# Which images of a normalised convolution take the combined path, and which engine measures them: four in eight and none on VectorE, to three in eight and one in eight on VectorE

## The chip, the cores and the metric

One Trainium2 chip, one core of it. The metric is the device time of one execution in microseconds (us). Engine names: PE is TensorE, DVE is VectorE, ACT is ScalarE, POOL is GpSimd, SP is SyncE, whose queue issues the loads and stores.

## The reference

`x` holds 160 images of 128 channels, 32x32 pixels, in f32. Images are dealt out to five weight sets (`b n` order, 32 images for each set). Every image is normalised over groups of four channels, run through a 3x3 convolution, and added to itself:

```
def _gn(v, G=32, eps=1e-5):                 # mean and variance of 4 channels x 32 x 32
    ...
    return ((g - m) / jnp.sqrt(s + eps)).reshape(v.shape)

# weights: U is quantised in two steps, s1 = (max - min)/3, s2 = s1/5
v1 = s1 * floor(U / s1);  v2 = s2 * floor((U - v1) / s2);  w = v1 + v2
x = x + conv3x3(_gn(x), w)                  # 128 -> 128 channels, padding 1, 5 weight sets
```

## The kernel before

**One image at a time.** Channels lie on the 128 partitions, an image is 1024 numbers on each. The normalised image is fed to PE in two f16 parts, a high part (the image rounded to f16) and a low part (what the rounding left), both multiplied by the same f16 weights. All weights are made beforehand, three columns of taps (`COLS`) for each weight set, and doubled, which is why the end multiplies by 0.5.

**Two paths for an image.** Two neighbouring output rows can share products: with the row differences, the pair sums and the pair differences of the input, four row products do the work of six. The kernel always feeds the low part in this form. The high part goes one of two ways:

- A *direct* image: ACT normalises it into f32 (`z`, L511) and rounds it (`hi`, L519). DVE subtracts (`lo`, L574) and builds the low part's differences and sums (`rows`, L588 to L591). PE runs the nine plain taps of `hi` (L614) and the shared products of `rows` (L640).
- A *combined* image: POOL writes two border rows (`outer_rows`, L539 and L540) and DVE the other differences and sums of the raw image (`combine`, `v`, L550 to L556). ACT scales and rounds all 2048 numbers (`vh`, L561), and DVE takes what is left (`vl`, L567). PE runs only shared products, of both parts (L640).

`combined(i)` (L522) says which: images 14 to 155 whose number modulo 8 is in `COMBINED`. With (1, 3, 5, 7) these are 71 of the 160 images; the other 89 are direct.

**PE's order.** `conv(i)` first issues the pair products of image i+1 into the PSUM tile `m` (`sums_of_pairs`), then the rest of image i into its tile `eo`. In between lie two small matmuls for each group's statistics (`means`, `variances`) and the turning of new weights (`turn_column`). `m` has one buffer and `eo` two, so before PE can start the pair products of image i+2, DVE must have read `m` of image i+1.

**What happens in stage i of the loop** (L857 to L961), engine by engine, in program order. The program is scheduled by hand: each engine runs its instructions in the order in which they are written.

- ACT: the first half of measuring image i+14, its sum (`image_sum`, L192); `sum` of image i-1, half of `eo` (L720); `m2` of image i+1, the copy of half of `m` (`leave`, L696); then `vh` or `z` and `hi` of image i+3; the second half of the measuring (`image_square`, L199); small operations for group statistics.
- DVE: the low part of image i+2 (`vl`, or `lo` and `rows`); one step of the next weight set's quantisation (`take(later, 1)`); `pairs` of image i+1 (L705, L706), which adds `m` and `m2` into `eo` and so frees `m`; then `combine` of image i+4 if that is a combined one, otherwise a second quantisation step; and last the measuring of those images that `by_vector` gives it.
- POOL: the transfer that adds `sum` to the image in SBUF (`accumulate`, L733); `outer_rows` of image i+4; the statistics of a group.
- SP: stores and loads, in units of two images; loads run 20 images ahead.

The lead of measuring is 14 images in the steady part and starts at about 10. Until stage 10 every second stage therefore measures two images instead of one. Statistics are made for groups of eight images (smaller groups at the start), two stages after the last image of a group is measured.

**Who measures.** `by_vector(i)` (L485) is true for images from 8 on whose number modulo 8 is in `MEASURED`; before, that tuple is empty. Such an image is measured on DVE by `Statistics.image` (L175): two `bn_stats` over 512 numbers, one `bn_aggr`, and two small multiplications, at the end of the stage.

Of the kernel before, what the change touches and what calls it, by code (L numbers as in the profile page):

```python
# [309 lines left out]
class Main:  # L310
# [24 lines left out]
    STAT_LEAD = 14  # L335
    LOAD_LEAD = 20
    STEADY = 14
    COMBINED = (1, 3, 5, 7)
    MEASURED = ()
    EARLY = 8  # L340
    FIRST = 3

# [142 lines left out]
    def by_vector(self, i):  # L485
        return i >= self.EARLY and i % 8 in self.MEASURED

# [34 lines left out]
    def combined(self, i):  # L522

        return self.STEADY <= i < self.imgs - LAST and i % 8 in self.COMBINED

# [485 lines left out]
```

## Time and profile before

| | |
|---|---|
| time, median of 3 runs | 1009.54 us (1009.02 to 1009.97) |
| the profiled execution's own time | 1009.54 us |
| its span in the profile | 1007.8 us, so 1.7 us lie around the span |
| mean granted PE clock | 0.995 of full |
| busy time PE, DVE, ACT, POOL | 964.8, 886.5, 931.2, 369.5 us |
| weight loads of PE (PEld) | 575.6 us |
| images combined, direct | 71, 89 |
| images measured by ACT, by DVE | 160, 0 |

The busy time of an engine is the union of its instructions' times. Matmuls overlap each other in the profile, so the pace of PE is read from start to start and not from the length of a matmul. The profiled execution took the median time, so a sum that starts from 1009.54 us stands for both.

### The profile page before, as it was taken

The page shows a single profiled execution, that of the slowest core. Times are in us where ns is not written, and L with a number is a line of the kernel's source. Part 1 is how long each engine was busy: PE and PEld are TensorE (multiplying, and loading weights), DVE is VectorE, ACT ScalarE, POOL GpSimd, SP SyncE. Part 2 cuts the span into 40 slices and gives each one's busy share as a digit, 9 for nine tenths or more (in the row PEclk, how much of TensorE's full clock was granted, in tenths as well). Part 3 has the DMA queues.
Part 4 walks back from the last instruction along what each step waited for, and adds up shares of the span by engine and source line. Part 5 has one row for each costly group of instructions (what it writes and reads, how often), then busy time and mean ns, then how long its engine had stood idle before and what let it go on. Part 6 is the DMA issues. An engine that isn't in the chain of part 4 may idle for free.

```text
span 1007.8 us, 15892 instructions
## 1 busy us (share of the span) xinstructions
PE 964.8 (96%) x5910; PEld 575.6 (57%) x5910; DVE 886.5 (88%) x1197; ACT 931.2 (92%) x1279; POOL 369.5 (37%) x555
## 2 busy tenths in 40 slices
PE   1879999999999999999999999999999999999997
PEld 0435456665666665666666566666665666666663
DVE  7956689999999999989999999999999988888873
ACT  4899999999999999999999999999999999998660
POOL 3413162534425243524243444415243623333210
PEclk9989999999999999999999999999999999999999
DMA  9627889999999999999999999999999999997763
GB/s 361 238 84 188 210 233 260 261 260 270 270 274 293 272 270 261 257 274 286 269 290 260 266 265 277 291 286 262 264 254 262 289 266 275 268 256 191 180 176 129
DMA packets 67287, 254.42 MB, mean 252 GB/s; under 512 B 5248, under 2 KB 5248, under 8 KB 67200
## 3 DMA queue, kind: packets, MB, share of 16 engines
q1 hardware_dynamic: 45168, 173.09, 50.4%
q0 software_dynamic: 22032, 80.23, 40.9%
q8 instruction: 48, 0.79, 0.3%
q14 instruction: 39, 0.32, 0.1%
HBM read 89.19 MB, written 83.89 MB: 172 GB/s over the span
## 4 chain that ended last, share of the span: by engine, by line
PE 88%; ACT 7%; issue 2%; DVE 1%; POOL 1%; DMA 1%; SPq 0%
PE eo L614 30%; PE eo L640 28%; PE m L640 28%; ACT junk L199 2%; ACT z L511 1%; ACT junk L192 1%; ACT hi L519 1%; ACT sum L720 1%; DMA range<-in_L_conv_U_dram 1%; DVE ext L422 1%; DVE ext L423 1%; ACT m L696 0%; PE pg L225 0%; PE m L614 0%; PE pg L208 0%
## 5 line engine op out<-in xcount | busy, mean ns | idle before, releaser
L640 PEld LDWEIGHTS <-wt 128*128 128x128 f16 x4104 | 400.3, 98 | 240.1 <-DVE rows L590 7.8
L614 PE MATMUL eo<-hi,wt 128*128 128x496 f16 (+3 forms) x1584 | 381.8, 377 | 1.1 <-ACT wt L476 1.1
L733 POOL DMA_DIRECT2D xt<-sum x153 | 135.9, 888 | 462.8 <-ACT sum L720 443.1
L614 PEld LDWEIGHTS <-wt 128*128 128x128 f16 x1656 | 162.9, 100 | 156.7 <-issue 4.5
L199 ACT ACTIVATE junk<-xt,mv 128x1024 f16<-128x1024 f32 x160 | 183.3, 1146 | 0.4
L192 ACT ACTIVATE junk<-xt 128x1024 f16<-128x1024 f32 x160 | 169.1, 1057 | 14.1 <-DMA xt<-in_x_dram 10.7
L705 DVE TENSOR_TENSOR eo<-m,m 128x512 f32<-128x512 f32 x157 | 109.2, 696 | 76.2 <-ACT m L696 75.8
L567 DVE SCALAR_TENSOR_TENSOR vl<-v,rstd,vh 128x2048 f16<-128x2048 f32 x71 | 166.7, 2348 | 3.5 <-ACT vh L561 3.5
L720 ACT ACTIVATE sum<-eo 128x1024 f32<-128x1024 f32 x153 | 154.1, 1007 | 12.9 <-PE eo L640 12.9
L640 PE MATMUL eo<-vl,wt 128*128 128x248 f16 (+1 forms) x852 | 162.9, 273 | 0.0
L640 PE MATMUL eo<-vh,wt 128*128 128x248 f16 (+1 forms) x852 | 162.9, 273 | 0.0
L640 PE MATMUL m<-vh,wt 128*128 128x496 f16 (+1 forms) x426 | 161.8, 380 | 0.0
L640 PE MATMUL m<-vl,wt 128*128 128x496 f16 (+1 forms) x426 | 161.7, 380 | 0.0
L640 PE MATMUL eo<-rows,wt 128*128 128x248 f16 (+1 forms) x1032 | 155.6, 273 | 0.0
L561 ACT ACTIVATE vh<-v,rstd 128x2048 f16<-128x2048 f32 x71 | 143.0, 2014 | 0.0
L640 PE MATMUL m<-rows,wt 128*128 128x512 f16 x516 | 127.0, 383 | 9.5 <-DVE rows L590 7.3
L706 DVE TENSOR_TENSOR eo<-m,m 128x512 f32<-128x512 f32 x157 | 109.8, 700 | 5.4
L574 DVE TENSOR_TENSOR lo<-z,hi 128x1024 f16<-128x1024 f32 x89 | 108.9, 1224 | 5.9 <-ACT hi L519 5.8
L511 ACT ACTIVATE z<-xt,shift,rstd 128x1024 f32<-128x1024 f32 x89 | 110.7, 1244 | 1.3 <-POOL shift L242 1.3
L696 ACT COPY m<-m 128x512 f32<-128x512 f32 x157 | 91.2, 581 | 20.4 <-PE m L640 17.8
L519 ACT CAST hi<-z 128x1024 f16<-128x1024 f32 x89 | 93.0, 1045 | 2.8
L550 DVE TENSOR_TENSOR v<-xt 128x960 f32<-128x960 f32 x71 | 81.7, 1150 | 0.0
(105 smaller groups left out, 804.3 us busy)
## 6 DMA issues: line engine op xcount, KB each, us to landing
xt<-in_x_dram SPq DMA_DIRECT2D x78, 1024.0 KB, 9.1
out_dram<-xt SPq DMA_DIRECT2D x78, 1024.0 KB, 5.0
xt<-sum POOLq DMA_DIRECT2D x153, 512.0 KB, 6.8
range<-in_L_conv_U_dram SPq DMA_DIRECT2D x4, 576.0 KB, 6.9
u<-in_L_conv_U_dram SPq DMA_DIRECT2D x4, 576.0 KB, 11.5
xt<-in_x_dram SPq DMA_DIRECT2D x4, 512.0 KB, 9.4
out_dram<-xt SPq DMA_DIRECT2D x3, 512.0 KB, 3.0
u<-in_L_conv_U_dram SPq DMA_DIRECT2D x2, 288.0 KB, 3.1
```

The costliest lines, as they stand in the source:

```text
L192: self.nc.scalar.activation(junk, image, ACTF.Copy, scale=-1.0 / image.shape[1], accum_out=self.mv[:, j, 0:1],)
L199: self.nc.scalar.activation(junk, image, ACTF.Square, bias=self.mv[:, j, 0:1], accum_out=self.mv[:, j, 1:2],)
L511: nc.scalar.activation(z, self.image(i), ACTF.Identity, bias=st.shift[:, j : j + 1], scale=st.rstd[:, j : j + 1],)
L561: self.nc.scalar.mul(vh, self.v[i], st.rstd[:, j])
L567: self.nc.vector.scalar_tensor_tensor(vl, self.v[i], st.rstd[:, j], self.hi[i], ALU.mult, ALU.subtract)
L574: self.nc.vector.tensor_sub(lo[:, 1 : self.H + 1, :].rearrange("p h w -> p (h w)"), self.z.pop(i), self.hi[i].rearrange("p h w -> p (h w)"),)
L614: nc.tensor.matmul(target[:, h, r0 - h0 : r1 - h0, c0:c1], self.wts[n, col][:, k, :], tile[:, s0 : s0 + r1 - r0, c0 + dw : c1 + dw], start ...
L640: self.nc.tensor.matmul(target[:, :, c0:c1], self.wts[n, col][:, kind, :], source[:, :, c0 + dw : c1 + dw], start=start, stop=stop, skip_g ...
L705: nc.vector.tensor_add(rows[:, :, 0], m[:, 0], m2)
L706: nc.vector.tensor_sub(rows[:, :, 1], m[:, 0], m2)
L720: nc.scalar.mul(self.sum[i], eo, 0.5)
L733: self.nc.gpsimd.dma_start(self.image(i), self.sum.pop(i), accum_op=ALU.add)
```

## The change

Two constants of the class `Main` change; nothing else in the file does.

```
-    COMBINED = (1, 3, 5, 7)
-    MEASURED = ()
+    COMBINED = (1, 4, 6)
+    MEASURED = (5,)
```

By the rules above, 53 images are combined and 107 direct (71 and 89 before). Images 15, 17, 19, 21 and so on used to alternate with direct ones; now the pattern of eight is direct, combined, direct, direct, combined, direct, combined, direct, starting with image 14. Images 13, 21, 29 and so on to 157, 19 in all, are measured on DVE and no longer on ACT.

## The prediction

> **What bounds the kernel now.** I began with the page's busy times and the chain that ended last.
>
> ```profile
> PE 964.8 (96%) x5910; PEld 575.6 (57%) x5910; DVE 886.5 (88%) x1197; ACT 931.2 (92%) x1279; POOL 369.5 (37%) x555
> PE 88%; ACT 7%; issue 2%; DVE 1%; POOL 1%; DMA 1%; SPq 0%
> ```
>
> Three engines are nearly full, and PE carries 88% of the chain. With engines this close, I need to know which one sets the pace of a pair of images, so I read the timeline for the start of each piece of PE's work: pair products of a direct image, rest of a combined one, pair products of a combined one, rest of a direct one, and the next piece.
>
> ```profile
> 514.95 1.46 PE L640 MATMUL m<-rows,wt 128*128 128x512 f16 x6
> 516.25 0.38 PE L640 MATMUL eo<-vh,wt 128*128 128x256 f16 x2
> 518.88 0.38 PE L640 MATMUL m<-vh,wt 128*128 128x512 f16 x1
> 521.47 1.43 PE L614 MATMUL eo<-hi,wt 128*128 128x512 f16 x6
> 526.59 0.60 PE L640 MATMUL m<-rows,wt 128*128 128x512 f16 x2
> ```
>
> From start to start: 1.30, 2.63, 2.59 and 5.12 us. A direct image costs PE 1.30 + 5.12 = 6.42 us, a combined one 2.59 + 2.63 = 5.22, a pair 11.64. Is that PE's own pace, or does ACT hold it there? The end of the run answers: from about 915 us on there is nothing left to measure, and ACT waits.
>
> ```profile
> 925.84 1.02 ACT L720 ACTIVATE sum<-eo 128x1024 f32<-128x1024 f32 x1 [2.72 <-PE eo L640]
> 937.62 1.02 ACT L720 ACTIVATE sum<-eo 128x1024 f32<-128x1024 f32 x1 [2.64 <-PE eo L640]
> 949.26 1.02 ACT L720 ACTIVATE sum<-eo 128x1024 f32<-128x1024 f32 x1 [2.64 <-PE eo L640]
> ```
>
> ACT sits idle 2.6 us before each of these, and still the pair takes 937.62 to 949.26 = 11.64 us. So PE is the bound, and ACT was only just keeping up. In the start-up it was the other way about. PE's timeline there shows the only waits after 70 us:
>
> ```profile
> 100.81 1.47 PE L640 MATMUL m<-rows,wt 128*128 128x512 f16 x6 [0.26 <-DVE eo L706]
> 107.92 1.47 PE L640 MATMUL m<-rows,wt 128*128 128x512 f16 x6 [0.52 <-DVE eo L706]
> 115.12 1.47 PE L640 MATMUL m<-rows,wt 128*128 128x512 f16 x6 [0.61 <-DVE eo L706]
> 122.23 1.47 PE L640 MATMUL m<-rows,wt 128*128 128x512 f16 x6 [0.52 <-DVE eo L706]
> 129.43 1.47 PE L640 MATMUL m<-rows,wt 128*128 128x512 f16 x6 [0.30 <-DVE eo L706]
> ```
>
> These are direct images, 7.0 to 7.2 us apart instead of 6.42. DVE is named, but it had waited for ACT's `m2`, and ACT runs without a gap here because it measures three images in two stages.
>
> **Part 1: 18 images become direct.** 71 - 53 = 18 images cost PE 6.42 - 5.22 = 1.20 us more each. All of them lie where PE sets the pace (it has no wait after 136 us), so nothing hides it: **+21.6 us**. The small matmuls for statistics and weights stay as many. POOL loses 18 times two border rows (0.70 + 0.82 us); POOL is 37% busy, so that is worth nothing.
>
> **Part 2: 19 images leave ACT.** The rows of what goes, of the nearest row to what comes, and of the quantisation step used below:
>
> ```profile
> L199 ACT ACTIVATE junk<-xt,mv 128x1024 f16<-128x1024 f32 x160 | 183.3, 1146 | 0.4
> L192 ACT ACTIVATE junk<-xt 128x1024 f16<-128x1024 f32 x160 | 169.1, 1057 | 14.1 <-DMA xt<-in_x_dram 10.7
> L422 DVE TENSOR_REDUCE ext<-u 128x1 f32<-128x576 f32 x2 | 1.5, 748 | 2.8 <-DMA u<-in_L_conv_U_dram 2.8
> L422 DVE TENSOR_REDUCE ext<-range 128x1 f32<-128x1152 f32 x4 | 5.4, 1346 | 0.6 <-DMA range<-in_L_conv_U_dram 0.6
> L109 DVE SCALAR_TENSOR_TENSOR tt<-nn,s2nlo,tt 128x384 f32<-128x384 int16 x15 | 9.2, 613 | 0.1
> ```
>
> With the accumulator reads (0.19 each, half hidden), a measured image takes ACT about 2.4 us, so ACT gives up 19 x 2.4 = 46 us and gets back 18 x 0.3 (`z` and `hi` take 2.2 us from start to start, `vh` 1.9). In the steady part that only lengthens ACT's waits. In the start-up it counts. Images 13 and 21 are measured in stages 3 and 8, before and inside the stretch that ACT holds; they take 4.8 us out of ACT's chain, of which about 0.5 is lost at once because ACT catches up with PE. PE's stages 7 to 13 run from 93.97 to 143.02, 49.05 us; as pure work they are 7 x 6.42 + 0.6 for statistics and one turned column = 45.5. ACT's credit of 4.3 exceeds this 3.5, so the gain is PE's whole excess, less a little for a stage that does not close up: **-3.3 us** (bounds 0 and -3.5). What is late next is PE itself.
>
> **Part 3: DVE's new measuring.** The trace has no `bn_stats`. By the two reduce rows an element costs (1346 - 748)/576 = 1.04 ns, so 512 elements 0.68 us; two of them 1.36. The three small operations go by the 128x1 rows of the start (0.15 us, 0.06 to 0.12 from start to start). Bounds: 2 x 0.44 + 0.2 = 1.1 us (each like the f16 subtraction of 512, 439 ns) and 2 x 1.35 + 0.5 = 3.1 us (each as long as the 1152-element reduce). I take 1.6, near the f32 reduce. It comes last in stages with i mod 8 = 7, and behind it are the low part of image i+3 and all else that PE waits for. Its image was loaded six images, over 30 us, earlier and lands in 9 us, so it should wait for no transfer. Per eight images DVE has 3 x 4.62 (combined) + 5 x 2.41 (direct) + 8 x 1.33 (`pairs`) + 1.6 = 38.2 us and up to 13 quantisation steps of 0.54, 45.2 in all, against PE's 5 x 6.42 + 3 x 5.22 + 0.55 = 48.3. On average DVE has room.
>
> **Part 4: the new rhythm.** A stage of PE is the rest of image i and the pair products of i+1. Before, long (5.12 + 2.59 = 7.71 us) and short stages (2.63 + 1.30 = 3.93) alternated. Now residues 0 to 7 take 7.71, 3.93, 6.42, 7.71, 3.93, 7.71, 3.93, 6.42. Each `pairs(i+1)` has to end before stage i+1 begins. The order on ACT and DVE in residues 4 to 6 is the tight place, and I add it from start-to-start times of the timeline:
>
> - Stage 4 is short, with 6.27 us on ACT after its `sum` starts: 1.34 to `m2`, 0.46, `z` 1.27, `hi` 0.95, the square 1.20, the next sum 1.05. ACT enters stage 5 late by 6.27 - 3.93 = 2.34.
> - In stage 5 `sum` (0.91) and `m2` (0.59) let `pairs` start 3.84 after the stage; DVE goes on with `pairs` 1.33, `combine` 2.36, the direct low part for stage 6 at 2.41, a quantisation step 0.54, `pairs` again 1.43, and 0.12 until PE takes it: 12.03.
> - Stages 5 and 6 last 7.71 + 3.93 = 11.64 on PE.
>
> So PE waits about 0.4 us for `pairs` where a quantisation step lies in between. Steps run through roughly 26 of 32 images of the first four sets, which hits stages 22, 38, 46, 54, 70, 78, 86, 102, 110 and 118: ten waits, **+4.0 us**. Without the step there is none, and with steps of 0.35 to 0.71 us it is 0.2 to 0.6, so 2 to 6 us. A second tight place, stage 1, follows DVE's unbroken run from there; it comes to 29.7 us against PE's 29.7, and costs nothing unless the measuring takes longer than 1.6. This stage's wait would be the one that appears next.
>
> Sum: 1009.5 + 21.6 - 3.3 + 4.0 = **1031.8 us**.
>
> One rule speaks against reading it like this. The Trainium skill, "Perfetto Trace Analysis", section "Identifying the Most-Contended Engine", says that matmul busy time is no measure of how full PE is and that the load of weights is, and to work on the engine with the highest occupancy. By that, PE stands at 57%, ACT at 92% is the one to relieve, and taking 46 - 5 = 41 us from it would give about 968 us. I take neither busy figure for PE, but the distance from start to start, which stays at 11.64 us when ACT is idle.
>
> **Rivals.**
>
> - *No new wait on PE.* If ACT enters stage 5 earlier than I added, the ten waits vanish: 1009.5 + 21.6 - 3.3 = 1027.8. For it: 0.4 us is small against the sums it comes from. Against: I dropped nothing that would make it shorter. 20%.
> - *DVE becomes the bound in the measured stages.* If the measuring takes 2.6 us instead of 1.6, stage 1 waits 1.0 us more in the ten blocks with quantisation steps, giving 1042; if the start-up gain is also missed, 1045. For it: 45 of 48 us are already full. 10%.
> - *Faster: ACT is the bound.* Then PE has slack to take the 1.20 us, and the run goes with ACT's 41 us, to 968. The point from which it decides is a direct image that costs PE less than 3.3/18 = 0.18 us more than a combined one, since otherwise the added PE work outweighs the start-up. The trace shows 1.20. 2%.
> - *Nothing moves.* The change was described as another order on ACT and POOL and a last image taken bank by bank; the diff has none of this, only two tuples. If the images taken from the combined path did not reach PE's chain, the time would stay at 1009.5. The chain is 88% PE, so 1%.
>
> **How the numbers follow.** The forecast of 1031.8 has 67%. The range of 1026.5 to 1039 takes in the case without waits and the bounds of the waits and the start-up, and leaves out the long measuring, both small rivals and mishaps that I did not think of. A measurement of this kernel tells 0.2%, about 2 us, from no change: faster 0.02, same 0.01, slower 0.97.
>
> **What would show it.** L561 with 53 instances and L511 with 107; a stretch of eight images at 48.3 us instead of 47.0, with PE at 100% and ACT near 92%; ACT waiting on PE before `sum` all along; no wait of PE for L706 between 100 and 130 us, and about ten of 0.2 to 0.6 us later. `bn_stats` at about 0.68 us. It would be wrong if ACT stayed gapless, if PE showed repeated waits of 1 us for L590 or L706, or if the eight-image stretch stayed at 47.

## The result, and the profile after

The changed kernel took 1038.93 us (median; 1038.7 to 1040.11) against 1009.75 us for the kernel before in the same comparison: 1.0289 times as long, 95% interval 1.0271 to 1.0307. The forecast was 1031.8 us, in a range of 1026.5 to 1039.0. The sign and the mechanism were right, but the time lies only 0.07 us inside the upper edge of the range, and one of the four terms was less than half of what came. The profiled execution took 1038.94 us with a span of 1037.2, 29.4 us more than the span before.

The page's busy times and the chain that ended last, of the changed kernel:

```profile
PE 987.3 (95%) x5910; PEld 575.3 (55%) x5910; DVE 879.3 (85%) x1292; ACT 901.0 (87%) x1221; POOL 344.2 (33%) x519
PE 74%; DVE 12%; ACT 11%; issue 2%; DMA 1%; POOL 0%; SPq 0%; ACTq 0%; DVEq 0%
```

ACT is 30 us less busy and DVE 7, and the kernel is 29 us slower. PE's share of the chain fell from 88 to 74%: DVE and ACT now hold the chain in places. The start-up, in PE's timeline (start, duration), answers to the five waits of 0.26 to 0.61 us before:

```profile
94.87 1.46 PE L640 MATMUL m<-rows,wt 128*128 128x512 f16 x6
...
101.29 1.46 PE L640 MATMUL m<-rows,wt 128*128 128x512 f16 x6
...
107.71 1.46 PE L640 MATMUL m<-rows,wt 128*128 128x512 f16 x6
```

Those waits are gone, and direct images follow one another at 6.42 us. The waits of PE in the whole run (what waited, for whom, us, times, longest) and the groups of the new measuring and of ACT's `sum`:

```profile
PE m L640 <- DVE eo L706: 6.7, 11, 0.9
L182 DVE BATCH_NORM_STATS2 st<-xt 128x6 f32<-128x512 f32 x38 | 24.3, 681 | 0.0
L184 DVE BATCH_NORM_AGGREGATE both<-st 128x2 f32<-128x12 f32 x19 | 4.0, 209 | 0.7
L720 ACT ACTIVATE sum<-eo 128x1024 f32<-128x1024 f32 x153 | 155.3, 1015 | 38.4 <-PE eo L640 38.3
```

ACT now waits 38 us for PE before `sum` (13 before), and the list has eleven waits of PE for `pairs`, all of them after 190 us (shorter ones, of 0.15 us and less, are not in it). The signs named ahead came: `vh` (L561) has 53 instances and `z` (L511) 107, and eight images take 48.0 to 49.3 us instead of 47.0. One sign of being wrong, repeated waits of 1 us for L706, came near: four of the waits are 0.8 to 0.9 us in the list, and these stages last 0.95 to 1.05 us longer than their work.

To see where the span went I took, from PE's timeline, the start of every stage (its first pair product) and compared its length with the pieces of the prediction, 1.30, 2.63, 2.59 and 5.12 us, plus the small matmuls in it:

| part of the span | before | after | difference |
|---|---|---|---|
| up to stage 4 | 74.30 | 75.19 | +0.89 |
| stages 4 to 12 | 62.13 | 58.65 | -3.48 |
| stages 13 to 157 | 852.67 | 883.81 | +31.14 |
| the rest | 18.7 | 19.6 | +0.86 |

Of the 31.14, 21.6 is the work of 18 images, and 9.5 is left over. Added up stage by stage, the excess over work is 9.7 us, and it lies in 16 stages, all with i mod 8 = 6: 22, 30, 38 and so on to 142. The first and the last row are not shown to be the change's. PE runs the same instructions up to stage 4 in every kernel here that measures images 8 to 12 on ACT, and its stage 4 began anywhere from 74.3 to 76.6 us in their profiles. At the end both traces agree to 0.01 us until the last store is issued, 13.4 us after the start of stage 158; the 0.86 lies in the closing semaphores behind it.

### The profile page after: what moved, and what is told of

The parts are those of the page before. It is cut to its first block, busy times and chain, and to the rows that moved or that the text cites. A ratio compares the mean times of both kernels' runs of the same rounds, so it can differ in the third digit from the quotient of the medians.

```text
span 1037.2 us, 15844 instructions
## 1 busy us (share of the span) xinstructions
PE 987.3 (95%) x5910; PEld 575.3 (55%) x5910; DVE 879.3 (85%) x1292; ACT 901.0 (87%) x1221; POOL 344.2 (33%) x519
## 3 DMA queue, kind: packets, MB, share of 16 engines
q1 hardware_dynamic: 45168, 173.09, 49.3%
## 4 chain that ended last, share of the span: by engine, by line
PE 74%; DVE 12%; ACT 11%; issue 2%; DMA 1%; POOL 0%; SPq 0%; ACTq 0%; DVEq 0%
PE eo L614 34%; PE m L640 21%; PE eo L640 18%; ACT junk L199 2%; ACT z L511 2%; ACT m L696 2%; DVE lo L574 2%; DVE eo L706 2%; ACT hi L519 2%; DVE eo L705 1%; ACT sum L720 1%; ACT junk L192 1%; DVE v L550 1%; DVE rows L588 1%; DVE v L553 1%
## 5 line engine op out<-in xcount | busy, mean ns | idle before, releaser
L614 PE MATMUL eo<-hi,wt 128*128 128x496 f16 (+1 forms) x1908 | 458.7, 377 | 1.1 <-ACT wt L476 1.1
L640 PE MATMUL eo<-rows,wt 128*128 128x248 f16 (+1 forms) x1248 | 188.1, 273 | 0.0
L640 PE MATMUL m<-rows,wt 128*128 128x496 f16 (+1 forms) x624 | 153.4, 382 | 14.4 <-DVE rows L590 7.3
L192 ACT ACTIVATE junk<-xt 128x1024 f16<-128x1024 f32 x141 | 149.0, 1056 | 13.4 <-DMA xt<-in_x_dram 11.2
L511 ACT ACTIVATE z<-xt,shift,rstd 128x1024 f32<-128x1024 f32 x107 | 133.6, 1248 | 0.0
L567 DVE SCALAR_TENSOR_TENSOR vl<-v,rstd,vh 128x2048 f16<-128x2048 f32 x53 | 124.5, 2348 | 6.2 <-ACT vh L561 5.8
L640 PE MATMUL eo<-vh,wt 128*128 128x248 f16 (+1 forms) x636 | 121.6, 273 | 0.0
L640 PE MATMUL eo<-vl,wt 128*128 128x248 f16 (+1 forms) x636 | 121.6, 273 | 0.0
L640 PE MATMUL m<-vh,wt 128*128 128x496 f16 (+1 forms) x318 | 120.7, 380 | 0.0
L640 PE MATMUL m<-vl,wt 128*128 128x496 f16 (+1 forms) x318 | 120.7, 380 | 0.0
L706 DVE TENSOR_TENSOR eo<-m,m 128x512 f32<-128x512 f32 x157 | 109.8, 700 | 5.4
L561 ACT ACTIVATE vh<-v,rstd 128x2048 f16<-128x2048 f32 x53 | 106.4, 2007 | 0.0
L588 DVE TENSOR_TENSOR rows<-lo 128x1024 f16<-128x1024 f16 x104 | 71.6, 688 | 1.3
```

Source lines behind the costliest of these rows:

```text
L192: self.nc.scalar.activation(junk, image, ACTF.Copy, scale=-1.0 / image.shape[1], accum_out=self.mv[:, j, 0:1],)
L511: nc.scalar.activation(z, self.image(i), ACTF.Identity, bias=st.shift[:, j : j + 1], scale=st.rstd[:, j : j + 1],)
L567: self.nc.vector.scalar_tensor_tensor(vl, self.v[i], st.rstd[:, j], self.hi[i], ALU.mult, ALU.subtract)
L614: nc.tensor.matmul(target[:, h, r0 - h0 : r1 - h0, c0:c1], self.wts[n, col][:, k, :], tile[:, s0 : s0 + r1 - r0, c0 + dw : c1 + dw], start ...
L640: self.nc.tensor.matmul(target[:, :, c0:c1], self.wts[n, col][:, kind, :], source[:, :, c0 + dw : c1 + dw], start=start, stop=stop, skip_g ...
L706: nc.vector.tensor_sub(rows[:, :, 1], m[:, 0], m2)
```

## The experiments

Each was compared with runs of the kernel before on its own chip, which took 1011.1 us (first four), 1011.2 (next four) and 1010.8 (last two). The differences below are against these; for the changed kernel the difference is +29.2 us.

**The pattern alone.**

```
-    COMBINED = (1, 3, 5, 7)
+    COMBINED = (1, 4, 6)
```

> Only COMBINED changes to (1, 4, 6); ACT still measures all images. Theory A (the time after is 21.6 us of PE work, minus a start-up gain of 2.6 to 3.3 that comes from the measuring of images 13 and 21, plus about 9.7 us of waits in stages with i mod 8 = 6 that come from the pattern itself): the start-up gain is lost and the waits stay, so about 1041.5 us, 1040 to 1044, with PE's waits for L706 back at 100 to 130 us. Theory B (the waits come from the bn_stats on DVE): the waits vanish, about 1031 us.

Measured: 1042.41 us, 31.3 more; ratio 1.0305, interval 1.0288 to 1.0322. PE's timeline has the start-up waits again, for example

```profile
116.16 1.47 PE L640 MATMUL m<-rows,wt 128*128 128x512 f16 x6 [0.61 <-DVE eo L706]
...
123.27 1.47 PE L640 MATMUL m<-rows,wt 128*128 128x512 f16 x6 [0.52 <-DVE eo L706]
```

and the excess in stages 6 mod 8 is 9.7 us, stage for stage within 0.01 that of the changed kernel, plus 0.4 in stage 14. So the waits come from the pattern and not from `bn_stats`, which this kernel does not run.

**The measuring alone.**

```
-    MEASURED = ()
+    MEASURED = (5,)
```

> Only MEASURED changes to (5,); images 1, 3, 5, 7 modulo 8 stay combined. Theory A: PE's work stays, the start-up closes up by 2.6 to 3.3 us, DVE is at about 46.9 of 47.0 us for eight images and just fits: 1007 us, 1006 to 1011. Theory B: the measuring on DVE makes PE wait about 0.5 us in each of the 13 blocks of eight with quantisation steps: 1010 less 3 plus 6.5, 1013 or more.

Measured: 1017.12 us, 6.0 more; ratio 1.0053, interval 1.0037 to 1.0070. Theory A fell here. The start-up closed up (stages 4 to 12 took 58.64 us), but PE then lost 9.2 us from stage 13 on, 0.1 to 0.7 in each of 19 stages, most of them 1 mod 8. DVE's timeline around stages 23 to 25 of this kernel (start, duration) shows why:

```profile
200.73 1.15 DVE L550 TENSOR_TENSOR v<-xt 128x960 f32<-128x960 f32 x1
...
203.06 1.28 DVE L182 BATCH_NORM_STATS2 st<-xt 128x6 f32<-128x512 f32 x2
204.37 0.21 DVE L184 BATCH_NORM_AGGREGATE both<-st 128x2 f32<-128x12 f32 x1
...
204.75 1.22 DVE L574 TENSOR_TENSOR lo<-z,hi 128x1024 f16<-128x1024 f32 x1
...
208.15 0.70 DVE L706 TENSOR_TENSOR eo<-m,m 128x512 f32<-128x512 f32 x1
```

DVE has no gap from `combine` to the `pairs` that ends at 208.85, and PE starts stage 25 at 208.90. The measuring took 203.06 to 204.75 = 1.69 us, as estimated; but with four combined images in eight, DVE has no such 1.7 us to spare while quantisation steps run. The last such wait is in stage 121; the measuring goes on to stage 143, but the last quantisation is done, and there are no more. A sum of 46.9 of 47.0 us was no room at all: the order in which the work has to be ready left less than the mean.

**The start-up alone.** Only images 13 and 21 are measured on DVE:

```
-        return i >= self.EARLY and i % 8 in self.MEASURED
+        return i in (13, 21)
```

> As the kernel before, but images 13 and 21 alone are measured on DVE. Theory A: the whole start-up gain and nothing else, 1007 us (1006 to 1007.5), with no wait of PE for L706 between 100 and 130 us. Rival (ACT's credit is used up elsewhere, or the start-up gain in the changed kernel came from image 14 being combined): 1009 to 1010 us.

Measured: 1007.29 us, 3.8 less; ratio 0.9964, interval 0.9951 to 0.9977. Stages 4 to 12 took 58.65 us, the same as in the changed kernel to 0.01, and PE's timeline shows no wait between 70 and 160 us. The gain in the start-up comes from these two images.

**The quantisation step and the copies moved.** The changed kernel, with work put off and none left out:

```
-            take(later, 1)                     # between lo and rows
+            if i % 8 != 6: take(later, 1)      # in stages 6 mod 8: behind pairs
...
-            for column, pt in turned: ...      # two ACT copies of a turned column
+            if i % 8 != 4: ...                 # else in the next stage
```

> The changed kernel with two moves: in stages with i mod 8 = 6 the quantisation step in front of pairs goes behind pairs, and the two copies of a turned weight column on ACT (0.73 us) are put off by a stage where they would fall in a stage with i mod 8 = 4. No work is added or removed. Theory A (PE's waits there are ACT's lateness plus DVE's row of work): the waits of 9.7 us in 16 stages fall to about 16 x 0.16, so 1032 us (1031 to 1034). Rival (PE waits there for another reason, such as the single buffer of m alone): 1038 to 1039.

Measured: 1035.50 us, 24.4 more; ratio 1.0236, interval 1.0219 to 1.0253. That misses the expected 1031 to 1034: all excess was to fall to about 2.6 us, and it fell from 9.7 to 6.8. Stages 38, 46, 70, 78, 102 and 110 went to 0.16. But stages 22, 30, 54, 62, 86, 94 and 126 ended at 0.56 (118 at 0.84), and a few stages 1 mod 8 now take 0.2 too long: a copy that is put off from stage 4 to stage 5 makes ACT late for stage 6 instead. The next run tests that.

**The copies clear of both stages.** As above, with the copies held in stages 4 and 5, and the last column of a set finished two stages earlier so that its copies fall in a stage 3 mod 8:

```
-            if i % 8 != 4: ...
+            if i % 8 not in (4, 5): ...
...
-            if b == self.per_set - 4:
+            if b == self.per_set - 6:
                 run(later)
```

> As the run with the quantisation step and the copies moved, but the copies of a turned column now also stay out of stages with i mod 8 = 5, and the last column of a set is finished two stages earlier so that its copies fall elsewhere. Theory A: the eight waits of 0.56 us that were left in stages 22, 30, 54, 62, 86, 94, 118 and 126 go to 0.16, 3.2 us less than that run's 1035.5, so 1032 (1031.5 to 1034). Rival (those waits have nothing to do with the copies): 1035 to 1036.

Measured: 1033.48 us, 22.3 more; ratio 1.0217, interval 1.0200 to 1.0234. The eight stages went to 0.16 or to nothing, and PE's wait for L706 is gone from its list of waits. All excess is 3.3 us in 19 stages. By the differences that is 6.9 us back of the 29.2, with nothing but order changed.

**The square put off.** The changed kernel, with one ACT instruction moved and DVE's order as it was:

```
+            for k in put_off: self.measure(k, (1,))       # behind leave(i + 1)
+            put_off = []
...
+            if i % 8 == 4 and i > 12: put_off, by_scalar = by_scalar, []
             for k in by_scalar: self.measure(k, (1,))
```

> The changed kernel with one move on ACT and none on DVE: in stages with i mod 8 = 4 the square pass of measuring (1.2 us) is put off behind the next stage's copy of m2. Theory A (PE waits in stages 6 because ACT enters stage 5 late, at 2.3 us and at 3.1 us where a turned weight column is copied, and everything on DVE follows from there): pairs starts 1.2 us earlier in stage 5, all waits in stages 6 go to about 0.16, and the time falls by 7 us to 1032 (1031 to 1034). Rival (DVE's own row of work in stages 4 to 6 is the limit, whenever ACT comes): no change, 1038 to 1040.

Measured: 1034.52 us, 23.3 more; ratio 1.0226, interval 1.0209 to 1.0243. That is just outside the expected 1031 to 1034, since not all went to 0.16: the excess fell from 9.7 to 5.7 us, 0.31 to 0.35 in each stage 6 mod 8 but one. Moving ACT's work alone takes 4.0 of the 9.7 us away, with DVE's row of work as long as before, so that row by itself is not the limit. What is left is again ACT, now late for stage 6: DVE's timeline has

```profile
290.07 0.42 DVE L591 TENSOR_TENSOR rows<-lo 128x512 f16<-128x512 f16 x1
290.72 0.70 DVE L705 TENSOR_TENSOR eo<-m,m 128x512 f32<-128x512 f32 x1 [0.23 <-ACT m L696]
```

a wait of 0.23 us for `m2` in stage 38, where in the changed kernel DVE was the late one.

**Two of eight.** The kernel before with fewer combined images still, and a pattern without a late short stage:

```
-    COMBINED = (1, 3, 5, 7)
+    COMBINED = (1, 5)
```

> The kernel before with COMBINED = (1, 5): 35 combined images, 36 fewer than before, none measured on DVE, and no short stage that ACT enters late. Theory A (PE pays 1.20 us for each image that becomes direct, nothing else): 36 x 1.20 = 43.2 us more than the kernel before on the same chip, about 1053 to 1054, with no wait of PE for L706 after 140 us. Rival (part of the price came from the pattern's waits, not from PE's work): under 1048.

Measured: 1053.51 us, 42.3 more; ratio 1.0420, interval 1.0403 to 1.0438. Stages 13 to 157 took 895.49 us, 42.8 more than before for 36 images, 1.19 each, and no stage from 13 on shows any excess. This is the price of a direct image on PE without any pattern in it.

**A denser end.** Meant to beat both kernels:

```
+        if i >= 127: return i < self.imgs - LAST and i % 3 != 0     # combined
+        return i in (13, 21, 137, 143, 149, 155)                    # measured on DVE
-   x 12, wide 1, wide_parts 2, sums 4 buffers
+   x 11, wide 2, wide_parts 3, sums 3 buffers
```

> A version meant to beat both: the kernel before with images 13 and 21 measured on DVE, and from image 127 on, where no quantisation steps are left, two of three images combined (20 instead of 15), with four of these images measured on DVE; one more buffer each for v and vh, one less for the images and for sum. Theory A (PE's work sets the time where ACT and DVE keep up): 5 x 1.20 = 6.0 us less than with the start-up part alone, 1001 to 1003. Rival (ACT, at 16.1 of 16.9 us for three images, or the missing buffers hold PE up): 1005 to 1010.

Measured: 1039.43 us, 28.2 more; ratio 1.0292, interval 1.0246 to 1.0338. It was expected at 1001 to 1003 us, by its rival at 1005 to 1010, and failed twice. Up to stage 122 its order is that of the start-up run, so what is lost there comes with the changed buffer counts: single stages between 52 and 67 are up to 10.4 us too long, and ACT waits eight times for images:

```profile
ACT junk L192 <- DMA xt<-in_x_dram: 19.7, 8, 11.8
```

It was 10.7 us, twice, before. Which of the four counts did it is not shown. And in the dense end every third stage from 128 to 152 is 1.5 to 1.9 us too long, which is more than the 0.6 us that a pattern of three was to gain. I did not take the two causes apart further.

**More of the start-up.** As the start-up alone, and images 8 and 9 measured on DVE too; then image 11 as well:

```
-        return i in (13, 21)
+        return i in (8, 9, 13, 21)          # then: (8, 9, 11, 13, 21)
```

> The kernel before with images 8, 9, 13 and 21 measured on DVE and all others on ACT. In the start-up PE stands idle for 7.3 us at about 58 to 66 us while ACT measures images 8 to 10 ahead of m2 of image 3, and DVE waits. Theory A (ACT's measuring holds the start-up there too): ACT gives up 4.8 us more before m2 of image 3, DVE's residual of image 1 becomes the last to come, PE's wait shrinks by about 2 us and nothing else changes: 1.5 to 2.5 us below the run with 13 and 21 alone, a ratio to the kernel before of about 0.994. Rival (the four small transfers, or DVE's two bn_stats in front of its residuals, take ACT's place): no change against that run, 0.996 or more.

> As the run before it, with image 11 measured on DVE too. Theory A: ACT has no more to give in the start-up once PE runs at its own pace from stage 4 on, so the same time as with 8, 9, 13 and 21, within 0.2%. Rival: another 1 to 2 us less.

Measured: 1006.32 us, 4.5 less, ratio 0.9960, interval 0.9946 to 0.9974; and 1005.00 us, 5.8 less, ratio 0.9945, interval 0.9931 to 0.9959. Both beat both kernels, by 0.4 and 0.55% against the kernel before. By their times alone the first of them and the start-up run are not told apart: the intervals overlap, and its ratio of 0.996 is what its rival gave, not the 0.994 expected. The traces tell more. PE's longest wait after the start, for the low part of image 4, in the start-up run and then in the run with 8, 9, 13 and 21:

```profile
PE m L640 <- DVE rows L590: 7.3, 1, 7.3
```

```profile
PE m L640 <- DVE rows L590: 4.8, 1, 4.8
```

The two `bn_stats` pairs lie where DVE had waited. Stage 3 begins 2.4 us sooner after stage 2 (8.85 against 11.29 us), where about 2 us was expected. With image 11 added, the wait and the stages up to 12 are the same to 0.1 us, so that the 1.3 us between the medians of these two are not shown to come from it.

## Why the prediction was right, and what it missed

**Part 1, PE's price: right.** 18 x 1.20 = 21.6 us; the two-of-eight run gave 1.19 for each of 36 images. With that, the rival that took ACT for the bound is dead, and so is the reading of PE by its weight loads alone ("Perfetto Trace Analysis" in the Trainium skill, section "Identifying the Most-Contended Engine", which names them beside a second measure, MFU, that the prediction does not use): PEld fell from 57 to 55% and ACT's occupancy from 92 to 87%, and the time rose by 2.9%.

**Part 2, the start-up: right.** -3.3 was forecast, and stages 4 to 12 gave -3.48, PE's whole excess. The run with images 13 and 21 alone shows that they bring it.

**Part 3, the measuring on DVE: right in size, and free only in this pattern.** 0.681 us for a `bn_stats` against 0.68 estimated, 1.69 for the whole against 1.6. (At 1.04 ns an element, 512 elements are 0.53 us; the 0.68 holds also the 0.15 that the two reduce rows leave over, which the prediction does not say.) In the new pattern it costs nothing (the excess with and without it is the same), but only just: in stages 17, 25 and 49 PE starts 0.19 us after `pairs` ends, and it starts 0.06 us after where `pairs` holds it up. In the old pattern it costs 9.2 us. The two halves of the change are therefore not additive: +31.3 and +6.0 alone, +29.2 together.

**Part 4, the new rhythm: the right place, the wrong size.** This step failed: +4.0 us was forecast, 9.7 came. The ten waits that were forecast came to 7.0, and the six stages 6 mod 8 without a quantisation step, forecast as free, to 2.7. The profile shows the place and what was left out of the row of work. ACT, DVE and PE of the changed kernel in stages 20 to 22, the first of the large waits:

```profile
178.15 1.02 ACT L720 ACTIVATE sum<-eo 128x1024 f32<-128x1024 f32 x1 [0.46 <-PE eo L640]
...
183.30 0.47 ACT L476 ACTIVATE wt<-pt 128x384 f16<-128x384 f32 x1
183.67 0.48 ACT L477 ACTIVATE half<-pt 128x384 f16<-128x384 f32 x1
184.04 1.05 ACT L192 ACTIVATE junk<-xt 128x1024 f16<-128x1024 f32 x1
...
185.08 1.02 ACT L720 ACTIVATE sum<-eo 128x1024 f32<-128x1024 f32 x1
185.98 0.59 ACT L696 COPY m<-m 128x512 f32<-128x512 f32 x1
```

```profile
186.61 0.70 DVE L705 TENSOR_TENSOR eo<-m,m 128x512 f32<-128x512 f32 x1 [0.83 <-ACT m L696]
187.34 0.70 DVE L706 TENSOR_TENSOR eo<-m,m 128x512 f32<-128x512 f32 x1
187.95 1.15 DVE L550 TENSOR_TENSOR v<-xt 128x960 f32<-128x960 f32 x1
189.02 0.74 DVE L553 SCALAR_TENSOR_TENSOR v<-xt,twice 128x512 f32<-128x512 f32 x1
189.68 0.68 DVE L556 TENSOR_TENSOR v<-xt 128x512 f32<-128x512 f32 x1
190.28 1.22 DVE L574 TENSOR_TENSOR lo<-z,hi 128x1024 f16<-128x1024 f32 x1
191.42 0.61 DVE L110 SCALAR_TENSOR_TENSOR tt<-tt,s1r,nn 128x384 f32<-128x384 f32 x1
...
193.94 0.70 DVE L706 TENSOR_TENSOR eo<-m,m 128x512 f32<-128x512 f32 x1
```

```profile
177.95 1.46 PE L640 MATMUL m<-rows,wt 128*128 128x512 f16 x6
...
189.76 1.46 PE L640 MATMUL m<-rows,wt 128*128 128x512 f16 x6
...
194.70 1.47 PE L640 MATMUL m<-rows,wt 128*128 128x512 f16 x6 [0.85 <-DVE eo L706]
```

Stage 21 began at 182.04, and ACT's `sum` in it at 185.08: 3.0 us late, not 2.34. DVE waits 0.83 us for `m2` and then works without a gap through the two `pairs`, `combine`, the low part and the step, to 194.64. PE, at work through stage 22 for 3.93 us from 189.76, could have gone on at 193.69. The links are those of the prediction; the three errors are in what was counted:

- *The copies.* I summed ACT's row from a stage without the two copies of a turned weight column (L476 and L477, 0.74 us in all). Two of the three pairs of copies of a set fall in stages 20 and 28 of it, both 4 mod 8, or, the second in the first set, one stage later. So they raise four of the ten waits (stages 22, 54, 86, 118) to about 1.0 us, and make four waits that I had as free (30, 62, 94, 126, without a quantisation step in the way) of about 0.6. With the copies clear of these stages and the step moved, all eight go.
- *The mean step.* I took 0.54 us for a quantisation step. In stages 38, 70 and 102 it is the 0.73 us one (L125) and the excess is 0.69; in 46, 78 and 110 the 0.35 us one (L112), and it is 0.31. The row of work gave 0.59 and 0.21 for them.
- *The start of the row.* I counted from the start of stage 4, but ACT waits for PE there, and its `sum` starts 0.20 us later (178.15 after 177.95). Stages 36 to 38, which have no copies, show what that does:

```profile
275.98 1.46 PE L640 MATMUL m<-rows,wt 128*128 128x512 f16 x6
...
276.18 1.02 ACT L720 ACTIVATE sum<-eo 128x1024 f32<-128x1024 f32 x1 [0.46 <-PE eo L640]
...
279.90 0.38 PE L640 MATMUL m<-vh,wt 128*128 128x512 f16 x1
...
282.50 1.00 ACT L720 ACTIVATE sum<-eo 128x1024 f32<-128x1024 f32 x1
...
284.02 0.70 DVE L705 TENSOR_TENSOR eo<-m,m 128x512 f32<-128x512 f32 x1 [0.94 <-ACT m L696]
```

From `sum` to `sum` ACT takes 6.32 us, nearly the 6.27 that I had, but it enters stage 37 2.60 us late, and `pairs` starts 4.12 us after the stage and not 3.84. DVE's row behind it is 0.17 us shorter than I added, above all because PE starts 0.06 us after `pairs` and not 0.12, and because a step takes 0.07 less from start to start than it is long. So 0.1 us was missing from these waits. Without a step, `rows` follows `lo` by 1.25 us, where a step follows it by 1.14, so leaving the step out saves 0.11 less. Together this is why stages 134 and 142, with neither copies nor a step, are still 0.16 us too long.

By the prediction's own bounds the waits were to be 6 us at most. That the time still fell inside the range is in part luck: its upper edge also had room for a start-up gain of nothing, and the whole gain came.

The rival without any wait (1027.8) was wrong in all of them, and the rival in which DVE's measuring binds (1042) had its time nearly right for a reason that the run with the pattern alone refutes.

## What to carry to other kernels

Where three engines are 88 to 96% busy, read which one keeps its pace when another runs out of work; that told at once that relieving ACT by 30 us could not pay for 21.6 us on PE. A pattern that mixes long and short stages is only as good as its tightest chain, so sum the row of work over two or three stages with every occasional instruction in it (here two copies in every tenth stage or so), not with means, and from the time at which the first engine is really let go. Work is free on another engine only where that engine stands idle: the same measuring on DVE gained 3.5 us in the start-up and, in the old pattern, lost 9 in the steady part, and four or five images of it, well placed, beat both kernels.

## What the runs showed of the hardware that was not expected

A wait of PE costs 0.16 us more than its list says. Idle time is counted from the recorded end of the last product, and a product that nothing holds up starts 0.16 us before that end. So stage 22 lasts 1.01 us longer than its work where 0.85 is listed, and stages 46, 78 and 110 lose 0.3 us each with nothing listed. PE is not slow to start again: where `pairs` holds it up, it starts 0.06 us after `pairs` ends, however short the wait. In the run with the copies clear of both stages, on PE and DVE around stage 89:

```profile
595.76 1.46 PE L640 MATMUL m<-rows,wt 128*128 128x512 f16 x6
...
599.06 0.70 DVE L706 TENSOR_TENSOR eo<-m,m 128x512 f32<-128x512 f32 x1
...
599.82 1.47 PE L640 MATMUL m<-rows,wt 128*128 128x512 f16 x6
```

No idle time is listed, and the stage takes 4.06 us instead of 3.93. To see what a short wait costs, take the start-to-start time and not the list.

DVE's f16 additions and subtractions can slow down while POOL adds f16 tiles. In the changed kernel's timeline, on DVE and POOL in stage 21, and on DVE in stage 22:

```profile
184.56 0.65 DVE L590 TENSOR_TENSOR rows<-lo 128x512 f16<-128x512 f16 x1
185.13 0.64 DVE L591 TENSOR_TENSOR rows<-lo 128x512 f16<-128x512 f16 x1
...
192.55 0.41 DVE L590 TENSOR_TENSOR rows<-lo 128x512 f16<-128x512 f16 x1
```

```profile
184.24 0.69 POOL L478 TENSOR_TENSOR outer<-half 128x128 f16<-128x128 f16 x1 [2.94 <-ACT half L477]
185.00 0.49 POOL L479 TENSOR_TENSOR wt<-outer,half 128x128 f16<-128x128 f16 x1
```

0.65 instead of 0.41 us for the same shape. L591 overlaps the making of new weights on POOL in nine of its 104 instances, and these take 0.65 us on average against 0.42. Overlap alone does not do it: L590 overlaps it nine times too, and takes 0.65 us in five of them and 0.42 in the other four, where a single POOL addition (L478) overlaps it. It costs nothing in stage 21, since DVE waits for `m2` right after. The Trainium skill ("SBUF — State Buffer", section "Terms") says that the two engines share one pair of SBUF ports, and that the one that finds it taken stands still for the whole of the other's instruction. The trace agrees that they disturb each other, by 0.24 us in the slowed instructions; which of the two stood still it does not tell.
